# Local attention and group whitening on one core: the last sub-image taken by channel half

## The chip, the core and the metric

The kernel runs on one core of a Trainium2 chip. The core has a matrix engine (TensorE, PE in the profile, with its weight loads as PEld), three engines for elementwise work (VectorE or DVE, ScalarE or ACT, GpSimd or POOL), SyncE (SP), which here only issues transfers, and 16 DMA engines. Matrix products land in PSUM[...]; only VectorE and ScalarE bring them from there to SBUF. The metric is the time of the program on the device, in microseconds, as the median of several runs; the profile is of one execution.

## The reference

The input x has 4 images of 256 channels, 64 x 64 pixels. Two layers follow one another.

```python
k = conv7x7_dilated2(x, w1) + b1          # 256 -> 128 channels
k = conv1x1(k, w2) + b2                   # 128 -> 49
attn = softmax(k, axis=1)                 # 49 weights for each pixel
y = einsum('bkchw,bkhw->bchw', shifts(x), attn)   # weighted sum of 49 shifted pixels

x = y as (g=4 groups, 64 channels, all pixels of all images)
xc = x - mean
Sigma = EPS * I + xc xc^T / m             # one 64 x 64 matrix for each group
rTr = 1 / trace(Sigma);  S = Sigma * rTr;  P = I
for _ in range(5): P = 1.5 * P - 0.5 * (P P P) S
out = (P * sqrt(rTr)) xc * weight + bias
```

The whitening needs the moments of all pixels of all four images before the first result can be written. The four groups are independent of each other.

## The kernel before

The dilated convolution works on row and column parities, with a transform that saves products; it fills most of the 686 us and isn't touched. Softmax gives the 49 weights of each pixel; they are written to memory and read back as banded matrices (`band`, and `bandz` for the edge between the two row halves), so that the weighted sum of a sub-image is a product of a block of transposed pixels with a band.

There are 16 sub-images (n = 0 to 15, four for each image, by row and column parity). A sub-image is worked on in `first_half` and `second_half`, its two row halves (the argument `half`). `make_blocks` (L1243) transposes pixels on TensorE (L1250) and copies them out as xb (L1281) and as edge blocks xbz (L1272). `weighted_sum` (L1296) adds one of five pieces of a row half into the PSUM tile y (L1313): four block pieces and an edge piece, each for the 128 channels `cc` = 0 and for `cc` = 1. These are the channel halves, two groups each. `store_y` (L1323) adds a pivot and puts y in its slot: ScalarE for channel half 0 (L1334), VectorE for half 1 (L1332) in the last three sub-images. `turn_y` (L1340) transposes the stored y again (L1346) and copies it to a buffer yt (L1356); `moments` (L1361) multiplies it with itself (L1371) and sums everything into the PSUM tile `sig`, which holds both channel halves side by side. A sub-image's second row half is turned, and its moments taken, within the next one's first row half; for the last, `finish` (L1402) does it.

After that `whiten(cc)` (L1629) is a generator, cut into steps by `yield`. From `sig` it forms the mean, the trace and S, then runs four rounds of two products with an eviction each (L1634 and L1685 are the copy and the update that ends a round), and at the end the scale and the offset (`sc`, `beta`). For channel half 0, `run_on` (L1622) puts products of the unit matrix into a PSUM tile `still` between the steps. The first step of half 1 comes after half 0's first round; its others are taken one by one in the output loop by `others`.

The output loop goes through the channel halves and images. It makes 32 tiles of 128 channels x 16 rows: products of the whitening matrix with the slots (L1615), for the two row parities; one is evicted by ScalarE (L1757), one by VectorE (L1761), into a ring of six SBUF tiles (tag `out`), and SP stores the tile (L1764). The PSUM pairs rotate over `apply` (both banks of one tile), `cv` and `tp` (two tiles each).

The order of TensorE's work is the order of the program (`pe` keeps it). A planner orders the work of the other engines by its estimates and by data; `high_priority` brings an instruction forward, and `issue_after` puts it behind another one. Each engine works off its own queue in order. The PSUM pool of y has one buffer, that of tp three.

## Time and profile before

| what | value |
|---|---|
| median of three runs | 688.17 us (687.89 to 688.29) |
| the profiled execution | 688.48 us, span 686.5 us |
| TensorE busy | 652.2 us (95% of the span) |
| VectorE / ScalarE busy | 567.1 us / 329.4 us |
| transfers of the result, L1764 | 32 of 512 KB, 5.7 us each from issue to landing |
| granted TensorE clock | 0.995 |

How to read it: times in the trace are microseconds from the start of the span. A row of the timeline has start, duration, engine, line, operation, result <- operands, shapes, count, and in brackets the idle time before it and what ended it. A row that gathers several instructions lasts from the first one's start to the last one's end. A float32 product is two instructions in the rows. A row of the chain has start, share of the chain in microseconds, engine, what and line; "issue" is time in which the engine waited for nothing that the profile shows. A busy TensorE isn't a TensorE doing needed work.

### The profile page before, as it was taken

To read this page: it belongs to the slowest core of one execution; us is meant where nothing else is said; L and a number is where in the kernel's file an instruction comes from. 1 tells how busy PE (TensorE), PEld (TensorE's weight loads), DVE (VectorE), ACT (ScalarE), POOL (GpSimd) and SP (SyncE) were. 2 spreads that over 40 slices of the span, in tenths; PEclk is the share of its full clock that TensorE was granted. 3 is DMA by queue.
4 is the path that set the end of the run, shared out by engine and by line. 5 is a ranking of instruction groups with operands and counts; after the bars stand their busy time and mean duration, and the time that the engine had idled before them with its cause. 6 is when DMAs were issued, how large, how long until landed. Compare 5 with 4: busy or idle time off the path is not lost.

```text
span 686.5 us, 19090 instructions
## 1 busy us (share of the span) xinstructions
PE 652.2 (95%) x7820; PEld 530.6 (77%) x7820; DVE 567.1 (83%) x1245; ACT 329.4 (48%) x849; POOL 117.4 (17%) x177
## 2 busy tenths in 40 slices
PE   6999999999999999999899999999999999999983
PEld 1439572367899998899899998999899998997320
DVE  2799999999489889999999499989998987433663
ACT  1424240023565564566754454464754656543463
POOL 0000551652222020002121200010220212400000
PEclk9999999999999999999999999999999999999997
DMA  8951999992699989222588493036462426646598
GB/s 318 246 155 66 143 265 354 219 182 38 151 192 220 209 194 365 86 90 74 151 267 275 108 325 116 6 94 169 137 177 73 98 48 155 166 147 284 223 405 353
DMA packets 110463, 126.09 MB, mean 184 GB/s; under 512 B 69239, under 2 KB 91880, under 8 KB 109224
## 3 DMA queue, kind: packets, MB, share of 16 engines
q1 hardware_dynamic: 93384, 69.03, 34.7%
q0 software_dynamic: 10944, 37.57, 21.7%
q10 hardware_dynamic: 6048, 18.27, 8.7%
q8 instruction: 61, 1.00, 0.6%
q14 instruction: 26, 0.21, 0.1%
HBM read 78.78 MB, written 52.36 MB: 191 GB/s over the span
## 4 chain that ended last, share of the span: by engine, by line
PE 68%; DVE 20%; ACT 6%; DMA 3%; issue 2%; DVEq 0%; ACTq 0%; POOL 0%; SPq 0%; POOLq 0%
PE cv L603 24%; PE y L1313 11%; PE cv L770 8%; PE acc L770 8%; PE tp L1346 3%; PE sig L1371 3%; PE tp L1250 3%; DVE pv L352 2%; DVE zz L352 2%; PE cv L251 2%; DVE xh L352 2%; DMA out_dram<-out 2%; DVE ct L352 2%; DVE zz L348 1%; DVE zz L345 1%
## 5 line engine op out<-in xcount | busy, mean ns | idle before, releaser
L603 PE MATMUL cv<-xh,wr 128*49 128x128 f32 x4160 | 232.5, 273 | 0.3 <-ACT pv L614 0.2
L603 PEld LDWEIGHTS cv<-xh,wr 128*49 128x49 f32 x4160 | 226.1, 124 | 3.4 <-issue 1.0
L1145 POOL DMA_DIRECT2D sd<-zt x124 | 65.4, 534 | 333.6 <-ACT zt L1126 268.5
L1313 PE MATMUL y<-band,xb 128*128 128x209 f32 x480 | 100.7, 342 | 5.3 <-ACT xb L1281 2.7
L1313 PEld LDWEIGHTS y<-band,xb 128*128 128x128 f32 x480 | 81.2, 191 | 6.6 <-ACT xb L1281 3.3
L614 ACT COPY pv<-cv 113x486 f32<-113x486 f32 (+2 forms) x60 | 25.9, 432 | 86.1 <-PE cv L603 85.8
L352 DVE SCALAR_TENSOR_TENSOR pv<-pv 113x162 f32<-113x162 f32 x176 | 52.8, 321 | 2.1 <-ACT pv L614 1.4
L1356 ACT COPY yt<-tp 128x512 f32<-128x512 f32 x64 | 37.2, 593 | 25.1 <-PE tp L1346 24.7
L1346 PE MATMUL tp<-ident,slot 128*128 128x128 f32 x256 | 45.5, 298 | 1.6 <-ACT slot L1334 1.2
L1126 ACT COPY zt<-d 32x112 f32<-32x112 f32 (+2 forms) x132 | 38.5, 291 | 15.5 <-DVE d L996 9.9
L1346 PEld LDWEIGHTS tp<-ident,slot 128*128 128x128 f32 x256 | 37.6, 206 | 7.8 <-issue 3.7
L1048 ACT ACTIVATE d<-tp,mx 128x49 f32<-128x49 f32 x96 | 27.5, 323 | 28.3 <-DVE mx L1045 28.3
L1250 PE MATMUL tp<-ident,slot 128*128 128x128 f32 x256 | 40.6, 282 | 0.0
L1371 PE MATMUL sig<-yt 128*64 128x65 f32 x1024 | 37.4, 225 | 1.8 <-ACT yt L1356 1.8
L1250 PEld LDWEIGHTS tp<-ident,slot 128*128 128x128 f32 x256 | 38.3, 206 | 0.2 <-issue 0.2
L1371 PEld LDWEIGHTS sig<-yt 128*64 128x64 f32 x1024 | 32.7, 137 | 6.3 <-ACT yt L1356 2.8
L352 DVE SCALAR_TENSOR_TENSOR xh<-ct 128x512 f32<-128x512 f32 x40 | 26.6, 693 | 10.3 <-PE cv L603 10.2
L1281 ACT COPY xb<-tp 128x512 f32<-128x512 f32 x52 | 30.6, 588 | 8.8 <-PE tp L1250 5.7
L770 PE MATMUL acc<-slot,tap 128*49 128x256 f32 (+7 forms) x224 | 34.7, 468 | 0.0
L770 PEld LDWEIGHTS acc<-slot,tap 128*49 128x49 f32 x224 | 16.1, 123 | 17.9 <-issue 15.5
L147 POOL DMA_DIRECT2D slot<-in_x_dram x12 | 20.4, 1701 | 54.1 <-DVE xh L352 38.6
L348 DVE TENSOR_TENSOR pv<-pv 113x162 f32<-113x162 f32 (+1 forms) x77 | 27.5, 365 | 0.3
(255 smaller groups left out, 1127.2 us busy)
## 6 DMA issues: line engine op xcount, KB each, us to landing
out_dram<-out SPq DMA_DIRECT2D x32, 512.0 KB, 5.7
band<-sd SPq DMA_DIRECT2D x64, 242.0 KB, 3.7
sd<-zt POOLq DMA_DIRECT2D x124, 77.0 KB, 3.2
wr<-gd ACTq DMA_DIRECT2D x14, 588.0 KB, 4.9
wr<-gd ACTq DMA_DIRECT2D x14, 490.0 KB, 5.3
slot<-in_x_dram POOLq DMA_DIRECT2D x12, 512.0 KB, 10.3
ahead<-in_x_dram POOLq DMA_DIRECT2D x12, 512.0 KB, 7.6
spill<-slot POOLq DMA_DIRECT2D x3, 2048.0 KB, 11.2
```

Of the source, the lines that this page charges most:

```text
L348: return in_turn(TT(o, a, b, ALU.subtract))
L352: return in_turn(STT(o, a, f, b, ALU.mult, ALU.add))
L603: nc.tensor.matmul(o, wv[:, sc, sr, cc], xv[bc][:, h * NCC + cc], start=(j == 0), stop=(j == len(terms) - 1), skip_group_check=True,)
L770: nc.tensor.matmul(ps[h * HB : h * HB + KT, :, o0:o1], w[v][:, cc], rhs, start=(j == 0 and k == 0), stop=(j == len(order) - 1), skip_group ...
L1126: ins = nc.scalar.copy(o, i)
L1145: dma = queue.dma_start(bass.AP(tensor=D.tensor, offset=D.offset + h * HS + g * RS, ap=[[LS, TC], [CR * RS, NCH], [1, KS * WS]],), zt[p0 : ...
L1250: nc.tensor.transpose(t[:, h * C + cc * P : h * C + (cc + 1) * P], tile_of(xt, cc, t8, h, pc), turned_by(n),)
L1281: (nc.vector.tensor_copy if n > 4 * B - 3 else nc.scalar.copy)(xb.rearrange("p a c -> p (a c)"), t[:, : 2 * C])
L1313: nc.tensor.matmul(ps[:, cc, q0 : q0 + nq, c0:c1], xb[:, cc * P : (cc + 1) * P], rhs, start=(k == 0), stop=(k == len(PIECES[half]) - 1), s ...
L1346: nc.tensor.transpose(t[:, h * C + cc * P : h * C + (cc + 1) * P], tile_of(yt, cc, t8, h, pc), turned_by(n),)
L1356: return nc.scalar.copy(yb.rearrange("p h a g c -> p (h a g) c")[:, :, :GW], t[:, : 2 * C].rearrange("p (e c) -> p e c", c=GW),)
L1371: nc.tensor.matmul(sig[g * GW : (g + 1) * GW, cc], yb[:, cc, g, :GW], yb[:, cc, g], start=(count[0] == 0), stop=(count[0] >= NCC * 4 * B * ...
```

## The change

The last sub-image (n = 15) gets an order of its own, by channel half. All weighted sums, turns and moments of channel half 0 come first, with two of the ten sums of half 1 behind the last turn. The rest of half 1 is cut into eleven units, which `whiten(0)` takes at the places where `run_on` stood; `run_on` and `still` go. Its y tile now holds the two row halves of one channel half, its block copies lie in tiles of the output ring so that they last, and stores and turned copies are split between ScalarE and VectorE (some units use one engine alone). Sub-images 13 to 15 order the copy of some blocks behind VectorE's store of y. In the whitening's start, two steps go to ScalarE and the sign of the mean moves; a square root is taken early, on a value that isn't used. The offset is made before the output loop. The first output tile is cut in two of 8 rows each, VectorE's first evictions are kept in order, and the second whitening starts behind output tile 4 and goes on by one step with each tile from number 6.

```diff
...
-    def make_blocks(n, t8):
+    LAST = 4 * B - 1
+    def make_blocks(n, t8, after=None):
...
                 )
-        if n == 4 * (B - 1):
+        if n in (4 * (B - 1), LAST):
             if t8 % 2 == 0:
                 ahead_xb.append(
-                    rpool.tile([P, 4, C], F32, tag="out", name=f"xbs_{t8}", bufs=6)
+                    rpool.tile([P, 4, C], F32, tag="out", name=f"xbs_{n}_{t8}", bufs=6)
                 )
...
             edges()
-        with tc.high_priority():
+        with tc.high_priority(), tc.issue_after(after.ins) if after else nullcontext():
             (nc.vector.tensor_copy if n > 4 * B - 3 else nc.scalar.copy)(
...
-    def weighted_sum(n, half, k):
+    def weighted_sum(n, half, k, ccs=range(NCC)):
         m = PIECES[half][k]
-        if k == 0:
-            y_ps[n, half] = ps_y.tile([P, NCC, HALF, SW], F32, tag="y", name=f"y_{n}_{half}")
-        ps = y_ps[n, half]
+        if n < LAST:
+            if k == 0:
+                y = ps_y.tile([P, NCC, HALF, SW], F32, tag="y", name=f"y_{n}_{half}")
+                for cc in ccs:
+                    y_ps[n, half, cc] = y[:, cc]
+        elif (half, k) == (0, 0):
+            y = ps_y.tile([P, 2, HALF, SW], F32, tag="y", name=f"y_{n}_{ccs[0]}")
+            for o in range(2):
+                y_ps[n, o, ccs[0]] = y[:, o]
         xb = blocks[n, m]
...
         yt, pc = where(n)
-        ps = y_ps.pop((n, half))
         shift = pivots[place(n)[1]]
...
             o = halves(yt)[:, cc, :, half * HALF : (half + 1) * HALF, bass.ds(pc, TC, 2)]
-            i = ps[:, cc].rearrange("p r (h c) -> p h r c", h=2)
+            i = y_ps.pop((n, half, cc)).rearrange("p r (h c) -> p h r c", h=2)
             with tc.high_priority():
                 if n > 4 * (B - 1) and cc:
-                    nc.vector.tensor_scalar(o, i, shift[:, cc : cc + 1], None, ALU.add)
+                    y_dve[n, half] = nc.vector.tensor_scalar(
+                        o, i, shift[:, cc : cc + 1], None, ALU.add
+                    )
                 else:
...
+    y_dve, y_act = {}, {}
+    def store_part(half, cc, both=True):
+        yt, pc = where(LAST)
+        shift = pivots[place(LAST)[1]][:, cc : cc + 1]
+        ps = y_ps.pop((LAST, half, cc)).rearrange("p r (h c) -> p h r c", h=2)
+        for h in range(2):
+            o = halves(yt)[:, cc, h, half * HALF : (half + 1) * HALF, bass.ds(pc, TC, 2)]
+            with tc.high_priority():
+                if h and both:
+                    y_dve[LAST, half] = nc.vector.tensor_scalar(
+                        o, ps[:, h], shift, None, ALU.add
+                    )
+                else:
+                    y_act[0] = nc.scalar.activation(o, ps[:, h], AF.Identity, bias=shift)
+    def turn_part(half, cc, to=None, on=(nc.scalar.copy, nc.vector.tensor_copy)):
+        yt, pc = where(LAST)
+        t = tp()
+        for k in range(4):
+            pe(
+                nc.tensor.transpose(
+                    t[:, k * P : (k + 1) * P],
+                    tile_of(yt, cc, 2 * half + k // 2, k % 2, pc),
+                    turned_by(LAST),
+                )
+            )
+        to = cc if to is None else to
+        for k in range(2):
+            with tc.high_priority():
+                on[k](
+                    yt_buf[k][:, :, to, :, :GW],
+                    t[:, k * C : (k + 1) * C].rearrange("p (h g c) -> p h g c", h=2, c=GW),
+                )
+        turned_part[half, cc] = [yt_buf[k][:, h, to] for k in range(2) for h in range(2)]
+    turned_part = {}
+    def moments_part(half, cc, pieces=range(4), end=False):
+        for k in pieces:
+            moment(turned_part[half, cc][k], cc, end and k == 3)
...
+    def moment(yb, cc, end=False):
+        for g in range(P // GW):
+            pe(
+                nc.tensor.matmul(
+                    sig[g * GW : (g + 1) * GW, cc],
+                    yb[:, g, :GW],
+                    yb[:, g],
+                    start=(count[0] == 0),
+                    stop=end,
+                    skip_group_check=True,
+                )
+            )
+        count[0] += 1
...
-        pieces = [(i, cc) for i in range(4 * half, 4 * half + 4) for cc in range(NCC)]
-        if (n, half) == (4 * B - 1, 1):
-            pieces.sort(key=lambda p: p[1])
...
+        for i in range(4 * half, 4 * half + 4):
+            for cc in range(NCC):
+                moment(ybs[n, i][:, cc], cc)
...
         load_band(n + 1, 0)
-        block(3)
+        make_blocks(n, 3, y_dve.get((n, 0))) if (n, (3, 0)) not in blocks else None
         if last is not None:
...
         if n + 1 < 4 * B:
-            make_blocks(n + 1, 0)
+            make_blocks(n + 1, 0, y_dve.get((n, 1)))
         moments(n, 0)
...
     soft_rows(1, 1)
-    for f in rest[5:]:
+    for f in rest[5:-2]:
         f()
-    finish()
+    def sums(half, cc, *ks):
+        for k in ks:
+            weighted_sum(LAST, half, k, (cc,))
+    prev = open_n.pop()
+    turn_y(prev, 2)
+    sums(0, 0, 0)
+    make_blocks(LAST, 1)
+    sums(0, 0, 1)
+    make_blocks(LAST, 2)
+    sums(0, 0, 2)
+    turn_y(prev, 3)
+    sums(0, 0, 3, 4)
+    store_part(0, 0)
+    make_blocks(LAST, 3, y_dve[LAST, 0])
+    moments(prev, 1)
+    root = work.tile([P, 1], F32, tag="root", name="root")
+    with tc.issue_after(y_act[0].ins):
+        nc.scalar.activation(root, cmask[:, :1], AF.Sqrt)
+    turn_part(0, 0)
+    sums(1, 0, 0, 1, 2, 3, 4)
+    store_part(1, 0)
+    moments_part(0, 0)
+    turn_part(1, 0)
+    sums(0, 1, 0, 1)
+    moments_part(1, 0, end=True)
+    units = [
+        lambda: sums(0, 1, 2, 3),
+        lambda: (sums(0, 1, 4), store_part(0, 1, False)),
+        lambda: sums(1, 1, 0, 1, 2),
+        lambda: sums(1, 1, 3),
+        lambda: (sums(1, 1, 4), store_part(1, 1)),
+        lambda: turn_part(0, 1),
+        lambda: turn_part(1, 1, 0, [nc.vector.tensor_copy] * 2),
+        lambda: moments_part(0, 1, (0, 1)),
+        lambda: moments_part(0, 1, (2, 3)),
+        lambda: moments_part(1, 1, (0, 1)),
+        lambda: moments_part(1, 1, (2, 3), True),
+    ]
...
-    still = ps_y.tile([P, 2, 512], F32, tag="y", name="still")
-    def run_on(k):
-        for _ in range(k):
-            pe(nc.tensor.matmul(still[:, 0, :P], ident, ident, start=True, stop=True))
-    latest = []
...
-        fill = run_on if cc == 0 else (lambda k: None)
+        def fill():
+            if cc == 0:
+                units.pop(0)()
...
         G = sig[:, cc]
-        mu = work.tile([P, 1], F32, tag="mu", name=f"mu{cc}")
-        nc.vector.tensor_scalar(mu, G[:, GW : GW + 1], 1.0 / NPIX, None, ALU.mult)
+        nmu = work.tile([P, 1], F32, tag="nmu", name=f"nmu{cc}")
+        nc.scalar.mul(nmu, G[:, GW : GW + 1], -1.0 / NPIX)
         D = small(f"D{cc}")
-        nc.vector.tensor_scalar(D, own, mu, None, ALU.mult)
-        if cc == 0:
-            t = tp()
-            fill(1)
-            pe(nc.tensor.matmul(t[:, :GW], blk, D, start=True, stop=True))
-        nmu = work.tile([P, 1], F32, tag="nmu", name=f"nmu{cc}")
-        nc.vector.tensor_scalar(nmu, mu, -1.0, None, ALU.mult)
+        nc.scalar.activation(D, own, AF.Copy, scale=nmu)
         dt_ = small(f"dt{cc}")
...
         nc.vector.tensor_reduce(dg, dt_, AX.X, ALU.add)
+        mu = work.tile([P, 1], F32, tag="mu", name=f"mu{cc}")
+        nc.vector.tensor_scalar(mu, G[:, GW : GW + 1], 1.0 / NPIX, None, ALU.mult)
         nc.vector.tensor_scalar(dg, dg, 1.0 / NPIX, EPS, ALU.mult, ALU.add)
         nc.vector.scalar_tensor_tensor(dg, mu, nmu, dg, ALU.mult, ALU.add)
+        fill()
         if cc:
             yield
-            t = tp()
-            pe(nc.tensor.matmul(t[:, :GW], blk, D, start=True, stop=True))
-        fill(2)
+        t = tp()
+        pe(nc.tensor.matmul(t[:, :GW], blk, D, start=True, stop=True))
+        fill()
         pe(nc.tensor.matmul(t[:, GW : GW + 1], blk, dg, start=True, stop=True))
...
         nc.vector.scalar_tensor_tensor(S, G[:, :GW], 1.0 / NPIX, eps, ALU.mult, ALU.add)
-        nc.vector.scalar_tensor_tensor(S, t[:, :GW], nmu, S, ALU.mult, ALU.add)
+        nc.vector.scalar_tensor_tensor(S, t[:, :GW], mu, S, ALU.mult, ALU.add)
         rtr = work.tile([P, 1], F32, tag="rtr", name=f"rtr{cc}")
...
     chains = [whiten(cc) for cc in range(NCC)]
-    for _ in range(3):
-        next(chains[0])
-    with tc.issue_after(latest[0].ins):
-        next(chains[1])
-    while 0 not in wm:
+    while 0 not in beta:
         next(chains[0])
...
-    def others():
-        for chain in chains:
-            if next(chain, "done") != "done":
-                break
+    LEAD = 4
+    evicted = {}
...
     pair = bank_pairs()
+    idx = -1
     for cc in range(NCC):
         for b in (3, 2, 1, 0):
-            for q in range(SH // TR):
-                st = rpool.tile([P, TR, 2, W], F32, tag="out", name=f"out_{b}_{cc}_{q}", bufs=6)
+            rows = [(q, TR) for q in range(0, SH, TR)]
+            if (cc, b) == (0, B - 1):
+                rows[:1] = [(0, TR // 2), (TR // 2, TR // 2)]
+            for k, (r0, nr) in enumerate(rows):
+                idx += 1
+                st = rpool.tile([P, TR, 2, W], F32, tag="out", name=f"out_{b}_{cc}_{r0}", bufs=6)
+                st = st[:, :nr]
                 ts = next(pair)
                 for pr in range(2):
-                    y = halves(slots[2 * b + pr])[:, cc, :, q * TR : (q + 1) * TR, :]
+                    y = halves(slots[2 * b + pr])[:, cc, :, r0 : r0 + nr, :]
                     parts_mm(
-                        ts[pr],
+                        ts[pr][:, : nr * W],
                         (wmx if pr else wm)[cc],
...
                     )
-                others()
+                if idx > LEAD + 1:
+                    next(chains[1], None)
                 for pr in range(2):
                     o = st[:, :, pr, :].rearrange("p r (h w) -> p h r w", h=2)
-                    i = ts[pr].rearrange("p (h r w) -> p h r w", h=2, w=SW)
-                    if pr == q % 2:
-                        nc.scalar.activation(
+                    i = ts[pr][:, : nr * W].rearrange("p (h r w) -> p h r w", h=2, w=SW)
+                    if pr == k % 2:
+                        on_act = nc.scalar.activation(
                             o, i, AF.Identity, bias=beta[cc], scale=sc[cc]
...
                     else:
-                        nc.vector.tensor_scalar(
-                            o, i, sc[cc], beta[cc], ALU.mult, ALU.add
-                        )
+                        behind = evicted.get(idx - 1) if idx <= LEAD else None
+                        with tc.issue_after(behind.ins) if behind else nullcontext():
+                            evicted[idx] = nc.vector.tensor_scalar(
+                                o, i, sc[cc], beta[cc], ALU.mult, ALU.add
+                            )
+                if idx == LEAD:
+                    with tc.issue_after(evicted[idx].ins), tc.issue_after(on_act.ins):
+                        next(chains[1])
                 nc.sync.dma_start(
-                    out[b, cc * P : (cc + 1) * P, 2 * q * TR : 2 * (q + 1) * TR, :],
+                    out[b, cc * P : (cc + 1) * P, 2 * r0 : 2 * (r0 + nr), :],
                     st.rearrange("p r two w -> p (r two) w"),
...
```

## The prediction

> **What bounds the kernel now.** I read the page first (TensorE busy 95% of the span, DMA 3% of the chain), then busy time by stretch over the last 86 us, the chain in order of time, and the timeline where the chain changes engine. Columns of the stretches: length, busy of PE, PEld, DVE, ACT, POOL, then clock, DMA share, GB/s.
>
> ```profile
> 625.00:630.00 5.00, 4.27 (x76) 3.45 (x70) 1.52 (x8) 2.94 (x4) 0.00 (x0) 1.00 0.85 364
> 630.00:635.00 5.00, 4.68 (x40) 3.54 (x41) 3.26 (x22) 0.73 (x3) 0.00 (x0) 1.00 0.04 16
> 635.00:640.00 5.00, 4.94 (x44) 2.58 (x44) 1.41 (x7) 0.87 (x4) 0.00 (x0) 1.00 0.00 0
> 642.00:644.00 2.00, 1.40 (x19) 0.58 (x22) 1.80 (x8) 0.61 (x2) 0.00 (x0) 1.00 0.89 363
> 646.00:648.00 2.00, 2.00 (x26) 0.72 (x24) 1.33 (x5) 1.58 (x3) 0.00 (x0) 1.00 0.81 315
> 656.00:676.00 20.00, 15.28 (x136) 4.92 (x136) 13.17 (x18) 11.45 (x17) 0.00 (x0) 1.00 1.02 406
> ```
>
> From about 642.2 to 684.3 us the transfers of the result (32 x 512 KB, 16.8 MB) run at about 405 GB/s; 16.8 MB at that rate is 41.4 us, so little is lost there. Nothing behind the first result byte can be shortened much; the end moves with the time of that byte. Ten microseconds before it the transfer engines are idle and TensorE is "busy". With what, the chain says:
>
> ```profile
> 628.27 0.94 PE sig L1371 x24
> ...
> 629.24 0.16 DVE mu L1638
> ...
> 632.39 0.42 PE still L1625 x2
> 632.81 0.27 PE tp L1615 x4
> 633.07 0.42 PE still L1625 x2
> ...
> 640.20 1.53 DVE out L1761 x2
> ```
>
> The last moment is in at 629.21; the whitening chain runs to the last update of its matrix (629.24 to 637.90, 8.7 us), with products of the unit matrix (`still`, L1625) filling TensorE; from 637.90 to the first byte (642.2) it is 4.3 us more. Two details of the timeline matter below.
>
> ```profile
> 605.47 0.69 DVE L1281 COPY xb<-tp 128x512 f32<-128x512 f32 x1 [1.03 <-PE tp L1250]
> 606.08 0.74 DVE L1332 TENSOR_SCALAR slot<-y,pivot 128x512 f32<-128x512 f32 x1
> 606.45 1.06 PE L1346 MATMUL tp<-ident,slot 128*128 128x128 f32 x4
> ...
> 624.85 0.74 ACT L1334 ACTIVATE slot<-y,pivot_x 128x512 f32<-128x512 f32 x1 [1.49 <-PE y L1313]
> 625.62 0.75 DVE L1332 TENSOR_SCALAR slot<-y,pivot_x 128x512 f32<-128x512 f32 x1 [5.25 <-ACT slot L1334]
> ...
> 628.24 1.28 ACT L1696 ACT_TABLE_LOAD   x1
> ```
>
> First: VectorE does the block copy before the store of y, and the transposes of y (1.06 us instead of 0.63) wait. Second: the two stores of y are strictly one after the other, though they read two banks of the tile y.
>
> **The change, part by part.** Half means channel half (0 or 1) here, as in the change's words.
>
> *Order of copy and store.* The block copy now follows VectorE's store of y. In the three places of sub-images 13 to 15 where both are on VectorE (598, 605.5, 611.8) the store starts at ScalarE's end instead of 0.35 to 0.75 later. At 606 the transposes then don't stall: 1.06 - 0.63, but only 0.33 after the overlap with the moments. At the other two the next sum waits for the later copy instead, so about 0.12 and 0.11 remain. What is queued behind the store is this copy; its readers are the next sums, and that is the loss just counted. For sub-image 13 the copy is on ScalarE and is read some 3 us later: nothing. Gain **0.55 us** (0 to 0.8).
>
> *Last sub-image by halves, before the whitening.* Pitches on TensorE: a block piece for both halves 0.71 (chain, 4 instructions), so 0.357 for one; an edge piece 0.42, so 0.21; four transposes 0.47; 32 moment instructions 1.1. Half 1's ten pieces are 8 x 0.357 + 2 x 0.21 = 3.28; two of them (0.71) stay ahead of the whitening, so 2.57 leave; with 8 transposes (0.94) and half of the moments (1.1) it is 4.6 us. The stalls change as well. Before, 619.99 to 629.21 holds 9.22 us for 7.4 us of work (16 transposes 1.9, sums 3.3, moments 2.2): 1.85 us of stalls. After, I lay it out: sums of half 0 end about 620.3 (on the old clock, without the gain above); store 0.51 on ScalarE (0.736 less 256 elements at the 0.83 ns that the rows of 512 and 256 elements, 587 and 367 ns, give) and then 0.48 on VectorE; 16 moments (0.55) cover part, so the transposes wait 0.5; their eviction (0.37 then 0.42, the 256-element rows of both engines) lies beside the two sums of half 1, with 0.2 left over. Stalls 0.7, 1.15 less. Up to the end of half 0's moments: **-5.75 us**, with the order -6.3.
>
> The copies of all four blocks now stay in two tiles of the output ring (six buffers, two were used before for sub-image 12): the ring is empty then, no wait.
>
> *The square root's table, placed early.* It is 1.28 us on ScalarE behind the store at about 617.5, before the eviction of the first half's transposes, ready 618.7: 0.3 late, with the sums (1.65 us) as cover, so nothing. The Trainium skill (ScalarE: Activation LUTs, What ACT_TABLE_LOAD costs) speaks against that: it puts a drain of about 1.38 us beside the load, 2.66 in all. ScalarE would then come free near 620.4, the eviction and the next store would shift, and the second transposes start 0.4 later. The trace shows only the 1.28 row, with ScalarE idle behind it until 631.29, so it can't exclude the drain; I take nothing and keep 0.4 for the range.
>
> *First whitening with real work as its filler.* 14 unit products (28 instructions, 0.42 us each product) go; 11 units come. Front: the first unit is 0.71; `D` now comes from ScalarE (two small ones, 0.2 and 0.24 by the rows of q and wmx) inside it; VectorE's sums on the diagonal wait for ScalarE's first reading of the same tile, then take about 0.9, ending near 1.15; unit two (0.21) ends there too. Before, the second product came 1.55 after the last moment; now 1.2. That gains 0.35.
> Unit two also issues two stores of half 1 on ScalarE, 1.0 us, from the lower bank of y, and unit three (0.92 us of sums) writes the upper bank of the same tile. The skill (PSUM — Partial Sum Buffer, PSUM bank collisions raise a hardware error) forbids two engines only the same bank in the same quadrant: by it unit three starts at once and the front keeps its 0.35. The trace shows more: at 624.85 and 625.62 two readers of *different* banks of one tile follow each other, and so do all pairs on the tile `apply`, never those on cv and tp, which are tiles of their own:
>
> ```profile
> 655.57 0.81 DVE L1761 TENSOR_SCALAR out<-apply,ab 128x512 f32<-128x512 f32 x1 [1.07 <-ACT out L1757]
> ...
> 663.32 0.78 ACT L1757 ACTIVATE out<-cv,ab 128x512 f32<-128x512 f32 x1 [0.45 <-DMA out_dram<-out]
> 663.63 0.80 DVE L1761 TENSOR_SCALAR out<-cv,ab 128x512 f32<-128x512 f32 x1
> ```
>
> If a matmul is held the same way (no row shows it), unit three starts 1.05 after unit two and the front *loses* 0.5. I take the loss, as the nearest row is that one; ends +0.35 and -0.5.
> Iterations: a step is now bound by the round trip (0.35 us from matmul end to the next matmul), not by 0.42 of filler; units of 0.36 and 0.28 fit, the two transpose units (0.47) don't (0.1 each), and the third iteration's bank of the ring of three waits for an eviction, 0.2. Against 5.95 before I take 6.15 (5.6 to 8.2, see the rivals). Whitening in all: **+0.7 us**.
>
> *First tile in two, offsets first.* After the last update: the offset's matmuls 0.3; half a tile of matmuls about 0.6 (half of 638.10 to 639.24); ScalarE 0.57, VectorE 0.54, one after the other as the tile is `apply`; with gaps 2.05; then 0.5 to the first byte as before (641.73 to 642.22). 2.55 against 4.3: **-1.75 us**. The offset is ready (0.8) before the matmuls are, so it is hidden. The second half follows 0.55 later, within the 0.65 that 256 KB take at 405 GB/s. SP issues one transfer more, 33 (0.7 us each), beside the stream.
>
> *Second whitening from tile 4 on.* Before it stole from VectorE while the stream was young (315 GB/s at 646); in all 0.7 us was lost. Now five tiles go first: by 0.8 us of eviction per tile against 1.29 of transfer the stream gains a lead of some two tiles before the first step. Gain **0.3** (-0.7 to +0.6).
>
> Sum: -6.3 + 0.7 - 1.75 - 0.3 = -7.65 us on the profiled execution (span 686.5, 688.48 with what lies around it). The median of the runs is 688.17, 0.3 below; I carry the difference over: **680.5 us**, span near 678.9.
>
> **Rivals.** (1) *Everything hides:* no hold on unit three, iterations at 5.6: 0.85 + 0.55 better, 679.1. For: the round trip 0.35; against: the serial readers. (2) *The evictions in the units become the chain:* the four units with stores or transposes put a 0.5 us item ahead of the chain's own copy or update in ScalarE's or VectorE's queue, each in its turn: +2.0, 682.5. For: both queues are in order and the stores come in the same microsecond as the copies; against: the chain's items are emitted first in most steps. (3) *Slower:* the second whitening starves the stream. Its eleven steps are tied to tiles 6 to 16, one each; a tile that takes over 1.29 us delays the last byte once the lead is used. To eat 7.65 us each of eleven must take 1.29 + 0.7 = 1.99 us; at 2.2 it is 11 x 0.91 = 10 us, 690.5. Against: with the steps in it before, 642 to 650 went at 366 GB/s, 1.43 us a tile. (4) *The change doesn't do what it says:* the readings of half 0's moments wait for half 1's as well, since both lie in one tile (`sig`); before, `mu` of half 0 started at 629.24 only after the last moment of half 1, at 629.21. Then only the first tile's 1.75 and the order's 0.55 are left, 685.9. Against: in the new program half 1's matmuls come behind those readings. The reloading of the slots isn't in the way: it ends near 629.5, five microseconds before the first byte.
>
> **How the numbers follow.** The case summed 0.55 (own range 679.6 to 681.5), (1) 0.18, (2) 0.22, (3) 0.03, (4) 0.02, half of which lies within 0.2%. The range goes from the low side of (1) to beyond (2), with the drain added: 678.8 to 683.3. A difference below 0.2% (1.4 us) can't be told from none here. Faster 0.96, same 0.01, slower 0.03.
>
> **What would show it.** Half 0's last moment near 622.9; the last update 9.4 later, at 632.3; first byte near 634.8; the stream then at 405 GB/s without a hole. The hold shows as TensorE idle 0.8 us ahead of unit three, released by ScalarE. No `still` rows. Wrong if the last update comes after 634 (case 2), or stretches under 370 GB/s lie between tiles 6 and 16 (case 3).

## The result and the profile after

The changed kernel takes **683.23 us** (five runs, 682.56 to 685.45) against 688.29 us (five runs, 687.89 to 690.32) for the kernel before, run beside it: a ratio of 0.9928, 95% interval 0.9904 to 0.9953. In a later group of runs on another chip it was 0.9945 (0.9921 to 0.9969). It is faster, by about 5 us instead of the 7.65 us that were forecast, and the time lies outside the range of the likeliest case and almost at the top of the wide one.

The profiled executions have spans of 686.5 and 681.3 us. To compare stretches I count from a marker that the change doesn't touch: the start of a block of 32 moment instructions of an earlier sub-image, near 569 us. It starts 0.42 us sooner in the profile after (569.02 against 569.44), which isn't the change's doing. All that follows is in distances from there. The first three stretches repeat to 0.05 us between executions of programs that are alike up to there; the last two are read from windows of a quarter of a microsecond, to about 0.1 us.

| stretch, us | before | after | change | forecast |
|---|---|---|---|---|
| marker to `dt`, an early reading of half 0's moments ("first reading" below) | 59.87 | 54.77 | -5.10 | -6.3 |
| front, to the first round's product | 2.64 | 3.22 | +0.58 | +0.5 |
| rounds, to the last update | 5.95 | 6.69 | +0.74 | +0.2 |
| last update to first byte | 4.28 | 3.07 | -1.21 | -1.75 |
| stream: first byte to the end of the full rate | 41.99 | 42.37 | +0.38 | -0.3 |
| sum | 114.73 | 110.12 | -4.61 | -7.65 |

Every row but the front has a share in the 3.0 us that are missing: 1.2, 0.5, 0.5 and 0.7. Three remarks on the rows:

- The very first reading (`mu` before, `nmu` after) lies 0.07 us ahead of `dt` before and 0.20 after. Counted from the end of the last moment, as the prediction counts, the first row is -5.2 and the front +0.7.
- The first packet of the result starts at 642.22 and 636.71, 4.32 and 3.02 us behind the last update: -1.30 by that count.
- The stream ends here where its full rate ends. Behind it comes a tail of 0.9 to 1.4 us, not the same in every execution, in which the DMA engines run empty (after: busy 47% in 679.00 to 679.25, 17% in the next quarter, then 6%). To the end of the last packet the change brings 4.76 us (115.79 to 111.03).

The chain of work that ended last, after, in the last sub-image and the whitening (start, share of the chain, engine, what, line):

```profile
613.75 0.70 DVE xbs L1282
...
614.48 0.37 ACT xbz L1273
...
620.42 0.50 ACT slot L1360
...
620.95 0.49 DVE slot L1356
...
622.82 0.72 PE sig L1418 x16
...
624.98 0.86 ACT slot L1360 x2
...
625.88 1.20 PE y L1320 x6
627.08 0.37 PE tp L1708 x4
627.45 0.55 PE y L1320 x2
...
629.18 0.67 PE tp L1368 x4
...
631.16 0.38 PE sig L1418 x8
...
633.80 0.22 PE tp L1708 x4
```

There is no `still` any more: its place is taken by sums (y, 0.55), transposes (tp L1368, 0.67) and moments (sig, 0.38). At 624.98 ScalarE's two stores are on the chain; that is the hold, TensorE's wait ahead of unit three. The timeline of the same execution shows the copies of blocks, the table load, the first reading, the hold and the first tile:

```profile
614.48 1.50 ACT L1273 COPY xbz<-tp 64x256 f32<-64x256 f32 x4 [1.15 <-DVE xbs L1282]
...
616.03 0.30 PEld L1320 LDWEIGHTS y<-bandz,xbz 128*128 128x128 f32 x2 [0.41 <-ACT xbz L1273]
...
617.04 1.28 ACT L1666 ACT_TABLE_LOAD   x1
618.33 0.20 ACT L1666 ACTIVATE root<-cmask 128x1 f32<-128x1 f32 x1
...
623.59 0.17 ACT L1724 ACTIVATE nmu<-sig 128x1 f32<-128x1 f32 x1 [1.01 <-PE sig L1418]
...
624.98 0.85 ACT L1360 ACTIVATE slot<-y,pivot_x 128x256 f32<-128x256 f32 x2 [0.84 <-PE y L1320]
...
625.88 0.46 PE L1320 MATMUL y<-bandz,xbz 128*128 128x96 f32 x2 [0.67 <-ACT slot L1360]
...
634.70 0.56 ACT L1837 ACTIVATE out<-apply,ab 128x256 f32<-128x256 f32 x1 [0.73 <-PE apply L1708]
...
635.30 0.54 DVE L1843 TENSOR_SCALAR out<-apply,ab 128x256 f32<-128x256 f32 x1 [0.81 <-ACT out L1837]
...
635.87 0.83 SPq L1849 DMA_DIRECT2D out_dram<-out  x2
```

Busy time by stretch (the columns are those of the prediction: length, PE, PEld, DVE, ACT, POOL, clock, DMA share, GB/s) shows two holes in the stream, at its start and at 646, and TensorE little busy at 642:

```profile
632.00:634.00 2.00, 1.96 (x39) 1.42 (x39) 0.79 (x4) 0.51 (x2) 0.00 (x0) 1.00 0.00 0
636.00:638.00 2.00, 2.00 (x20) 0.72 (x24) 1.83 (x3) 0.72 (x2) 0.00 (x0) 1.00 0.66 247
642.00:644.00 2.00, 1.16 (x17) 0.64 (x19) 1.64 (x7) 1.45 (x3) 0.00 (x0) 1.00 0.98 385
646.00:648.00 2.00, 1.77 (x21) 0.40 (x13) 2.00 (x6) 0.91 (x2) 0.00 (x0) 1.00 0.78 307
660.00:670.00 10.00, 8.09 (x76) 2.54 (x70) 7.01 (x9) 6.21 (x9) 0.00 (x0) 1.00 1.02 406
```

### The profile page after: what moved, and what is told of

It is laid out like the page before. It is cut to its first block, busy times and chain, and to the rows that moved or that the text cites. A ratio compares the mean times of both kernels' runs of the same rounds, so it can differ in the third digit from the quotient of the medians.

```text
span 681.3 us, 19062 instructions
## 1 busy us (share of the span) xinstructions
PE 648.7 (95%) x7800; PEld 527.3 (77%) x7800; DVE 568.4 (83%) x1248; ACT 330.4 (48%) x857; POOL 117.2 (17%) x177
## 4 chain that ended last, share of the span: by engine, by line
PE 66%; DVE 20%; ACT 6%; DMA 4%; issue 2%; POOL 0%; ACTq 0%; SPq 0%; DVEq 0%; POOLq 0%
PE cv L603 22%; PE y L1320 11%; PE cv L770 8%; PE acc L770 8%; PE sig L1418 4%; PE tp L1399 3%; PE tp L1251 3%; DVE pv L352 2%; DVE zz L352 2%; PE cv L251 2%; DVE xh L352 2%; DMA out_dram<-out 2%; DVE ct L352 2%; DVE zz L348 1%; ACT d L1048 1%
## 5 line engine op out<-in xcount | busy, mean ns | idle before, releaser
L1320 PE MATMUL y<-band,xb 128*128 128x209 f32 x448 | 94.0, 342 | 5.0 <-ACT xb L1282 2.7
L1320 PEld LDWEIGHTS y<-band,xb 128*128 128x128 f32 x448 | 75.7, 190 | 6.5 <-ACT xb L1282 3.3
L1409 ACT COPY yt<-tp 128x512 f32<-128x512 f32 x60 | 35.0, 593 | 19.4 <-PE tp L1399 19.0
L1399 PE MATMUL tp<-ident,slot 128*128 128x128 f32 x240 | 41.5, 296 | 1.2 <-ACT slot L1342 1.2
L1251 PE MATMUL tp<-ident,slot 128*128 128x128 f32 x256 | 40.5, 282 | 0.0
L1399 PEld LDWEIGHTS tp<-ident,slot 128*128 128x128 f32 x240 | 34.9, 205 | 6.3 <-issue 3.7
L1251 PEld LDWEIGHTS tp<-ident,slot 128*128 128x128 f32 x256 | 38.2, 204 | 0.2 <-issue 0.2
```

The costliest lines, as they stand in the source:

```text
L1251: nc.tensor.transpose(t[:, h * C + cc * P : h * C + (cc + 1) * P], tile_of(xt, cc, t8, h, pc), turned_by(n),)
L1320: nc.tensor.matmul(y_ps[n, half, cc][:, q0 : q0 + nq, c0:c1], xb[:, cc * P : (cc + 1) * P], rhs, start=(k == 0), stop=(k == len(PIECES[hal ...
L1399: nc.tensor.transpose(t[:, h * C + cc * P : h * C + (cc + 1) * P], tile_of(yt, cc, t8, h, pc), turned_by(n),)
L1409: return nc.scalar.copy(yb.rearrange("p h a g c -> p (h a g) c")[:, :, :GW], t[:, : 2 * C].rearrange("p (e c) -> p e c", c=GW),)
```

## The experiments

My theory after the result: the mechanisms are those of the prediction, and four of its terms have the wrong size. The rivals: the evictions in the units hold the rounds (case 2 of the prediction), and the stream is starved by the second whitening (case 3). The stretches of all runs, in us, counted as above; "full rate" is the distance from the marker to the end of the full rate, "last packet" that to the end of the last packet; the ratio is that to the kernel before in the same group of runs:

| run | first reading | front | rounds | first byte | stream | full rate | last packet | median, ratio |
|---|---|---|---|---|---|---|---|---|
| before | 59.87 | 2.64 | 5.95 | 4.28 | 41.99 | 114.73 | 115.79 | |
| after | 54.77 | 3.22 | 6.69 | 3.07 | 42.37 | 110.12 | 111.03 | 683.23, 0.9928 |
| e1_upper_in_cv | 54.75 | 2.50 | 6.68 | 3.06 | 42.36 | 109.35 | 110.31 | 682.81, 0.9912 |
| e2_units_first | 61.74 | 2.52 | 7.03 | 3.56 | 43.83 | 118.68 | 119.97 | 693.48, 1.0055 |
| e3_first_tile_whole | 54.76 | 3.22 | 6.69 | 3.88 | 42.71 | 111.26 | 112.53 | 683.51, 0.9912 |
| e4_order_alone | 59.11 | 2.64 | 5.95 | 4.30 | 41.93 | 113.93 | 115.04 | 687.29, 0.9986 |
| e5_units_first_filled | 61.75 | 2.61 | 5.94 | 3.03 | 42.39 | 115.72 | 116.85 | 688.97, 1.0018 |
| e6_no_second_whitening | 54.76 | 3.23 | 6.67 | 3.07 | 41.68 | 109.41 | 110.81 | 683.84, 0.9934 |
| e7_two_tiles_first | 54.79 | 2.49 | 6.69 | 2.51 | 42.56 | 109.04 | 110.25 | 682.54, 0.9913 |
| e8_small_units | 54.78 | 2.50 | 6.33 | 2.46 | 43.11 | 109.18 | 110.50 | 681.65, 0.9905 |
| e9_best | 54.67 | 2.50 | 6.33 | 2.47 | 43.92 | 109.89 | 111.17 | 686.17, 0.9951 |
| e10_second_from_tile_0 | 54.77 | 3.22 | 6.68 | 3.19 | 43.09 | 110.95 | 112.10 | 686.67, 0.9955 |
| e11_edges_ordered | 54.67 | 3.22 | 6.69 | 3.02 | 42.36 | 109.96 | 111.10 | 685.25, 0.9937 |
| a0_after (changed kernel again) | 54.78 | 3.22 | 6.68 | 3.08 | 43.76 | 111.52 | 112.46 | 685.24, 0.9945 |

Half widths of the ratios' intervals are 0.0010 to 0.0028, so most variants of the changed kernel can't be told apart by their times; the stretches can. In the last group the changed kernel's median is 2 us higher, which goes with TensorE's clock (last section): its executions with a mean granted clock of 0.995 or more took 683.5 and 684.0 us, those below 684.7 to 687.9.

**The hold.** The upper half of half 1's sums goes to a bank of the tile `cv`, which is a tile of its own, and no longer to the other bank of the tile y.

```diff
...
+            if ccs[0]:
+                y_ps[n, 1, 1] = cv_buf[0].rearrange("p (r c) -> p r c", c=SW)
```

> The sums of the upper row half of channel half 1 go to a PSUM tile of their own (the first cv tile) instead of the second bank of y. Theory (hold): a matmul is kept off a tile while another engine reads any bank of it; then the 0.67 us in which TensorE waited for ScalarE ahead of unit three is gone, the first round starts 0.85 us sooner after the last moment of half 0 (2.7 instead of 3.54 us), and the time is about 0.8 us below the changed kernel. Rival (the wait is for something else, the buffers of the transposes or ScalarE's queue): the wait stays, and the time is that of the changed kernel.

The front falls from 3.22 to 2.50, the time from the marker to the last packet by 0.72. The timeline of e1: the matmuls start 0.10 us after the stores instead of 0.90.

```profile
625.23 0.86 ACT L1362 ACTIVATE slot<-y,pivot_x 128x256 f32<-128x256 f32 x2 [0.84 <-PE y L1322]
...
625.33 0.44 PE L1322 MATMUL cv<-bandz,xbz 128*128 128x96 f32 x2
```

So a matmul waits for readers of another bank of the same tile (y is one tile of two banks, `cv` are two tiles of one bank each), and with that wait gone the front is 0.14 better than before, where the prediction had 0.35. The bank read and the bank written are different ones in both kernels, and what differs is the tile; that speaks for the framework's tracking of tiles as the cause, but these runs don't show it.

**Units ahead of the whitening, then with the old filler.** Both take the eleven units in one go before the whitening starts. The first leaves its rounds bare, the second fills them with products of the unit matrix as the kernel before did.

```diff
...
         def fill():
-            if cc == 0:
-                units.pop(0)()
+            pass
...
+    for f in units:
+        f()
     chains = [whiten(cc) for cc in range(NCC)]
```

> All eleven units stand ahead of the first whitening, which then runs with nothing between its steps. Theory (each filler costs its first weight load, 0.1 to 0.2 us, besides its matmuls): the four rounds take 5.5 to 5.7 us instead of 6.62, the front about 2.3 instead of 3.54, so the whitening is 2.2 us shorter; but the 5 us of matmuls and some 1 us of stalls come before it: first result byte about 3.5 to 4 us later than in the changed kernel, time near 687. Rival (the fillers are free and the rounds are bound by VectorE and ScalarE): the rounds stay above 6.4 us and the time is near 689.

```diff
...
+        counts = [1, 2, 3] + [1] * 8
+
         def fill():
             if cc == 0:
-                units.pop(0)()
+                for _ in range(counts.pop(0)):
+                    pe(nc.tensor.matmul(still[:, 0, :P], ident, ident, start=True, stop=True))
...
+    for f in units:
+        f()
+    still = ps_y.tile([P, 2, 512], F32, tag="y", name="still")
```

> As the kernel with the units ahead of the whitening, but with the old products of the unit matrix (14 of them, in the old places) between its steps, so that TensorE's clock has no cause to fall. Theory (the gain is the units' work under the whitening, and a filler costs its first weight load besides its matmuls): the clock stays at 1.00, the front takes 2.6 to 2.8 us and the four rounds 5.9 to 6.0, against 3.54 and 6.62 in the changed kernel; the units in a row cost 7.0 us, so the first byte comes 5.5 us later, time 688.5. Rival (what made the other kernel slow was not the clock but the units' stores in a row): the rounds stay above 6.6 us with the clock at 1.00.

The first missed its expectation by 6 us. Busy time by stretch of e2 says why: TensorE was at work 40% of 632 to 636 us, and then its clock was halved for ten microseconds (0.50 to 0.52 in all windows from 636 to 646).

```profile
632.00:634.00 2.00, 0.79 (x4) 0.59 (x4) 1.42 (x9) 0.49 (x2) 0.00 (x0) 1.00 0.00 0
634.00:636.00 2.00, 0.80 (x10) 0.45 (x10) 1.09 (x7) 0.32 (x2) 0.00 (x0) 1.00 0.04 8
636.00:638.00 2.00, 1.31 (x10) 0.73 (x12) 0.42 (x2) 0.27 (x1) 0.00 (x0) 0.52 0.00 0
```

The Trainium skill (TensorE: Matmul & The Clock Gate, What's actually happening) says that the clock is halved after an idle window of about 3.4 us; the 4 us here agree in length, though TensorE was partly at work in them. So a filler is needed, and e2 says nothing on the evictions. e5 does: clock 1.00, rounds 5.94, 688.97 us against 688.5 expected. The units cost the rounds 0.75 us (6.69 - 5.94). Comparing e5 with e4, the order by halves *costs* 2.64 us (61.75 against 59.11) as long as half 1's work stays ahead of the whitening, with the waits between its units in that sum; taking that work into the whitening brings 6.98.

**First tile whole.**

```diff
...
-            if (cc, b) == (0, B - 1):
-                rows[:1] = [(0, TR // 2), (TR // 2, TR // 2)]
```

> The first result tile is not cut in two. By the prediction's working half a tile saves 0.3 us of matmuls, 0.21 and 0.27 of evictions: the first byte comes 0.8 us later than in the changed kernel and the end with it, about 0.8 us more. Rival: the stream's first microseconds have slack in both kernels (holes of about 1 us lie between tiles 4 and 12), so that the later first byte is won back and the time is the same within 0.3 us.

The first byte comes 0.81 us later, and the stream is 0.34 longer; in that execution the clock fell at 643.0, with TensorE idle for 40% of 640 to 642 (busy time by stretch of e3):

```profile
640.00:642.00 2.00, 1.20 (x8) 0.80 (x12) 1.49 (x7) 1.29 (x2) 0.00 (x0) 1.00 1.01 399
...
644.00:646.00 2.00, 2.00 (x16) 0.76 (x13) 1.04 (x6) 0.26 (x1) 0.00 (x0) 0.50 1.03 397
```

In the medians the 0.8 us can't be seen (683.51 in its group).

**The order of copy and store alone**, in the kernel before:

```diff
...
-        block(3)
+        make_blocks(n, 3, y_dve.get((n, 0))) if (n, (3, 0)) not in blocks else None
...
-            make_blocks(n + 1, 0)
+            make_blocks(n + 1, 0, y_dve.get((n, 1)))
```

> The kernel before with only the block copies of sub-images 13 to 15 ordered behind VectorE's store of y. Prediction's step: 0.55 us faster than before, with the transposes at 599, 606 and 613 no longer waiting; it can hardly be told from none by the clock, but by the trace: first sum of sub-image 15 about 0.55 us earlier, counted from the last moments of sub-image 11. In sub-image 15's own second half nothing stands in VectorE's way. Rival: the later block copy delays the next sums by the same amount: 0.

0.9986 (0.9976 to 0.9996), and 0.76 us in the trace. Of these 0.32 are at a fourth place, within the last sub-image: four transposes at 619.99 took 0.90 from start to start in the kernel before and take 0.58 here. At the three places of the prediction it is 0.44.

**No second whitening.** Both channel halves use half 0's matrix, scale and offset: the whitening of half 1 is left out.

```diff
...
+    for table in (wm, wmx, sc, beta):
+        table[1] = table[0]
...
-                if idx > LEAD + 1:
-                    next(chains[1], None)
...
-                if idx == LEAD:
-                    with tc.issue_after(evicted[idx].ins), tc.issue_after(on_act.ins):
-                        next(chains[1])
```

> Leaves out the whitening of channel half 1: its tiles are made with half 0's matrix, scale and offset. Theory (the second whitening's steps hold TensorE and VectorE up in tiles 6 to 16, and the stream, whose lead is under two tiles, runs dry): the stretch of 307 GB/s goes, the stream takes 41.5 us from first to last byte instead of 42.4, time 682.4. Rival (the holes come from the transfers themselves, or from the serial evictions on the tile apply): the holes stay and the time is that of the changed kernel, 683.2.

The stream takes 41.68 instead of 42.37 us; the tail gives part of that back, and to the last packet it is 0.22 us. The median, 683.84, doesn't show the 0.7; in the profiled execution the clock fell at 334 us, ahead of the marker. All that the second whitening takes from the stream is thus 0.7 us or less. The stretch of 307 GB/s at 646, the sign that the prediction named for case 3, is there after the change and gone here (380 to 414 in all windows from 640 to 658), so case 3 is real in kind; in size, 7.65 us, it is refuted.

**The second whitening without a lead:** first step behind tile 0 instead of 4.

```diff
-    LEAD = 4
+    LEAD = 0
```

> The changed kernel with the second whitening's steps behind tiles 0 to 12 instead of 4 on. Theory that the lead of four tiles matters: the early steps take VectorE and TensorE from a young stream, which becomes longer, 42.6 to 43.2 us against 42.37, and the time 0.3 to 0.8 longer, 683.5 to 684.0. Rival, the steps cost the stream the same wherever they stand: 42.37 and 683.2.

The stream becomes 43.09, as the theory had it; the hole is at 642 (e10, busy time by stretch):

```profile
642.00:644.00 2.00, 1.96 (x27) 0.60 (x24) 1.68 (x6) 1.73 (x3) 0.00 (x0) 1.00 0.35 135
```

The lead is worth 0.72 us in this kernel (1.07 to the last packet). The medians (686.67 against 685.24 for the changed kernel in the same group) point the same way, but their intervals overlap.

**First tiles on separate PSUM tiles.** e1's edit, and the PSUM pairs come in the order cv, tp, apply.

```diff
...
         while True:
-            t = ps_y.tile([P, 2, NT], F32, tag="y", name="apply")
-            yield [t[:, k] for k in range(2)]
             yield cv_buf
             yield [tp(), tp()]
+            t = ps_y.tile([P, 2, NT], F32, tag="y", name="apply")
+            yield [t[:, k] for k in range(2)]
```

> The changed kernel with the upper row half of channel half 1 in the first cv tile, and the first two half tiles of the result on the pairs cv and tp, whose two banks are tiles of their own, instead of apply and cv. Theory (two readers of one PSUM tile are kept apart): ScalarE and VectorE evict the first half tile at once, the first byte comes 0.5 us sooner after the last update (2.5 us instead of 3.0), on top of the 0.72 of the separate tile: 1.2 us below the changed kernel's first byte, time 682.0. Rival (the later tiles then run dry, since the whole third tile now waits for the serial pair): the gain is lost in a hole behind the second half tile, time 682.7.

The two evictions of the first half tile now run side by side (timeline of e7; after, the same pair stood at 634.70 and 635.30), and the first byte comes 0.56 us sooner after the last update than in the changed kernel:

```profile
633.90 0.56 ACT L1839 ACTIVATE out<-cv,ab 128x256 f32<-128x256 f32 x1 [0.62 <-PE cv L1710]
634.02 0.54 DVE L1845 TENSOR_SCALAR out<-cv,ab 128x256 f32<-128x256 f32 x1 [0.21 <-PE cv L1710]
```

But the stream is 0.20 longer than e1's (42.56), with 206 GB/s from 636 to 638, and to the last packet only 0.06 of e1's time is gained: the rival of this run, a hole behind the second half tile, is in part right.

**Small units.** On top of e7: the two units of four transposes become four of two, and half 1's last moments go from the rounds to the place ahead of tile 3.

```diff
...
-        lambda: turn_part(0, 1),
-        lambda: turn_part(1, 1, 0, [nc.vector.tensor_copy] * 2),
+        lambda: turn_pair(0, 1, 0, 1),
+        lambda: turn_pair(0, 1, 1, 1),
+        lambda: turn_pair(1, 1, 0, 0),
+        lambda: turn_pair(1, 1, 1, 0),
...
-        lambda: moments_part(1, 1, (0, 1)),
-        lambda: moments_part(1, 1, (2, 3), True),
...
+                if idx == 2:
+                    moments_part(1, 1, range(4), True)
```

> As the one with two tiles first, and the units cut by what a step leaves free: transposes by twos (0.19 + 0.24 us) in four steps, evicted by ScalarE, moments of half 1's lower rows in two, and those of its upper rows behind the third tile's matmuls. Theory (a filler costs 0.19 us for its first weights besides its matmuls, and what exceeds the round trip lengthens the round): the second and third round take 1.5 us each instead of 2.0 and 1.45, all four 6.2 instead of 6.62, first byte another 0.4 sooner, time 681.6. Rival (rounds are bound elsewhere): 6.6 us, no change.

Rounds 6.33, and 681.65 us, the shortest median of all, though not apart from e7's. The chain of e8 shows a unit of two transposes and a unit of eight moments:

```profile
628.52 0.44 PE tp L1682 x2
...
631.67 0.38 PE sig L1420 x8
```

Two transposes cost 0.44, four 0.67. Four without interruption are 0.47, so there is a fixed price of 0.20 us, whatever the number of transposes; eight moments pay 0.10 (0.38 against 0.28). But the stream is now 43.11: from 636 to 638 us it moved 210 GB/s, and from 644 to 648 it moved 320 and 346. In the profile e8 ends 0.25 us later than e7; that execution was the slowest of its four.

**Everything together.** On top of e8: two tiles in halves instead of one, half 1's last moments behind tile 4, one more tile of lead, and e11's order of the edges.

```diff
...
-    LEAD = 4
+    LEAD = 5
...
-                rows[:1] = [(0, TR // 2), (TR // 2, TR // 2)]
+                rows[:2] = [(r, TR // 2) for r in range(0, 2 * TR, TR // 2)]
...
-                if idx == 2:
+                if idx == 4:
                     moments_part(1, 1, range(4), True)
```

> The small units and the first two tiles in four halves on cv, tp, apply; half 1's last moments behind the fifth tile instead of ahead of the fourth; the second whitening one tile later; the halves' edge pieces in the order of their use. Theory that the hole of 1 to 2 us just behind the first byte comes from the moments ahead of tile 3 and from the serial tile apply: stream 42.4 or less (43.11 in the run with small units before this one), first reading 54.5 (54.78), rounds 6.33, first byte 2.5 behind the last update: about 681.0 us, 2.2 below the changed kernel. Rival, the transfers themselves start slowly: the stream stays at 43.1 and the time at 681.5.

Both expectations missed: the early hole is gone, and two later ones took its place, so that the stream is longer still, 43.92 (busy time by stretch of e9):

```profile
636.00:638.00 2.00, 2.00 (x32) 1.06 (x32) 1.37 (x4) 0.78 (x2) 0.00 (x0) 1.00 0.99 365
...
640.00:642.00 2.00, 0.55 (x3) 0.42 (x4) 1.83 (x6) 1.18 (x3) 0.00 (x0) 1.00 0.81 326
...
644.00:646.00 2.00, 1.75 (x24) 0.57 (x20) 2.00 (x6) 1.24 (x3) 0.00 (x0) 1.00 0.29 104
```

The first byte is 65.97 us behind the marker, against 67.75 in the changed kernel, but the end of the full rate only 0.23 sooner, and the last packet 0.14 later. From e7 over e8 to e9 the first byte comes 0.4 and 0.1 us sooner and the end of the full rate 0.1 and 0.7 *later*: with fewer tiles ahead, it seems, the evictions around the second whitening's first step can't keep up with the transfers. The median is 686.17 beside 685.24 of the changed kernel in the same group: nothing gained. No version here has a shorter median than e8 and e7, and these two are not told apart from e1 by time or by last packet (110.25 to 110.50).

**The edges' order.** ScalarE copies the edge that half 0's sums need first ahead of the other one.

```diff
...
+                late = edge_of.get(2) if n == LAST and t8 == 1 else None
-                with tc.high_priority():
+                with tc.high_priority(), tc.issue_after(late.ins) if late else nullcontext():
```

> The changed kernel with one order more: ScalarE copies the edge that half 0's sums need before the one that half 1's need. Theory that the halves' order uncovered this copy: the edge piece no longer waits, and the first reading of half 0's moments comes 54.5 us behind the moments of sub-image 11 (54.77 in the changed kernel); 682.9 us. Rival, the wait only moves to the next eviction: 54.75 and 683.2.

In between: 0.10 us of the hoped-for 0.27. The sum's edge piece comes straight behind the sum now, and part of the wait goes to the next transposes (timeline of e11):

```profile
616.04 0.35 PE L1321 MATMUL y<-bandz,xbz 128*128 128x96 f32 x2
...
616.41 0.74 PE L1251 MATMUL tp<-ident,slot 128*128 128x128 f32 x4
```

**The changed kernel again**, without an edit, beside e9 to e11:

> The changed kernel once more, beside the others of this group. Both theories: about 683.2 us, ratio 0.9928; the stretches as in its first profile: moments of sub-image 11 to the first reading of half 0's moments 54.8 us, front of the whitening 3.22, rounds 6.69, last update to first byte 3.07, stream 42.4.

All stretches up to the first byte repeat to 0.01 us. The stream doesn't, 43.76 against 42.37, and the marker comes 2.98 us later. Together these are the 4.4 us between the two spans (685.7 and 681.3), and both go with falls of the clock, as the last section shows.

## Why the prediction was partly wrong

**Last sub-image by halves: the term "stalls 0.7, 1.15 less" failed.** The work that leaves was right: from start to start of the rows, the sums' stretch shrinks by 3.18 us from e4 to the changed kernel where whole pieces and transposes make 3.75, and the rest by 1.24 where they make 0.84. The 0.7 us of stalls that I laid out behind the sums measured 0.87. What I left out lies *ahead of* them: between 612.62 and 616.91 the sums now lose 0.66 us in waits of 0.1 to 0.24, and in e4 0.11. With both halves a piece lasts 0.71 us and covers a copy of a block (0.69 on VectorE), and the chain of e4 stays on TensorE from 610.9 to 623.6; with one half it lasts 0.36, and the chain after goes through VectorE's copy at 613.75 and the four edge copies on ScalarE (1.50 us at 614.48), for whose end the edge piece waits at 616.03. That these copies are behind all of the 0.66 is argued: e11 moved one of them and won 0.10. So the stalls from e4 on are 0.55 more and 0.40 less, not 0.83 less. (0.32 of the 1.15 is the order's fourth place, e4.) This is the largest miss, 1.2 us in the table's first row with 0.1 of the order and 0.1 for `dt`, which stands later behind the last moment. (Two slips in the working: the rows named for 0.83 ns an element give 0.86, and 9.22 less 7.4 is 1.82. The first store measured 0.49 against 0.51; neither matters.)

**Order of copy and store.** 0.55 forecast, 0.44 at the places named: right. It brought 0.32 more at a place that the prediction didn't see (e4).

**The front.** The hold was foreseen rightly, from the nearest row, but the sum fits better than its parts: 0.85 was taken for the hold, and e1 takes 0.72 away; the 0.35 to be gained ahead of it came out as 0.14, and as 0.03 when counted from the last moment. +0.5 forecast and +0.58 measured agree in part by luck. The rule of the Trainium skill weighed there (PSUM — Partial Sum Buffer, PSUM bank collisions raise a hardware error) would have let unit three start at once, since it writes another bank; the row at 625.88 and e1 decide for the wait.

**Rounds: "units of 0.36 and 0.28 fit" failed.** They don't: their pitch isn't their price. The chain through the rounds lies on TensorE alone, but for 0.04 us twice, so it is not the evictions either (case 2). The last update came at 633.70, 1.4 after the forecast and just ahead of the 634 that was to show case 2; that the time came out 0.7 from case 2's 682.5 is chance. A sum unit takes 0.55 instead of 0.36, four transposes 0.67 instead of 0.47, eight moments 0.38 instead of 0.28. Against eight times 0.42 of `still` that is 2 x 0.55 + 2 x 0.67 + 4 x 0.38 = 3.96, or +0.6 of the measured 0.74; the third bank's wait of 0.2 didn't show. e8 shows the price of transposes to be fixed for each unit. What it is stays open. The matrix chain uses 64 x 64 quarters of the array and the units more of it, and the Trainium skill (TensorEngine Tiling (Array Packing), Key Properties) says that a change of tiling mode drains TensorE, without a figure. The expectations of e2, e5 and e8 name a rival, the first weight load of a unit, and it fits the sizes as well: the loads of sums, transposes and moments last 0.19, 0.21 and 0.14 us on the page of the kernel before. No run here parts the two. The old filler paid it too: it took 0.42 for two instructions of 128 columns, and four such instructions take 0.47 in the transposes. So I had the price in front of me and read it as the filler's own length.

**First byte: the step "then 0.5 to the first byte as before" failed.** I measured from the eviction that ended at 641.73, that of `apply`. SP's queue sent the tile from `cv` first: its evictions ended at 641.35, the issue is at 641.38, ahead of the end of `apply`'s, and the first packet started at 642.22, 0.87 us behind the eviction (timeline of before):

```profile
640.58 0.77 ACT L1757 ACTIVATE out<-cv,ab 128x512 f32<-128x512 f32 x1
...
640.93 0.80 DVE L1761 TENSOR_SCALAR out<-apply,ab 128x512 f32<-128x512 f32 x1
...
641.38 0.81 SPq L1764 DMA_DIRECT2D out_dram<-out  x2
```

After, it is 635.84 to 636.71, 0.87 again. The evictions themselves ended 2.14 after the last update, forecast 2.05. The two together, 0.46, are the whole miss when the first packet is counted (3.02 against 2.55).

**Second whitening from tile 4: "gain 0.3" failed.** The stream lost 0.38. The lead does help (e10: 0.72), but the whitening's first steps used to run within the first whitening and around the first byte and now stand in the stream, 2.5 to 6 us behind it: TensorE is busy 1.16 of 2 us at 642. I counted the steps by tile and not what was moved. Without the whitening the stream would take 41.68 (e6), so the most to gain was 0.3 against before, all of which the forecast claimed. That the place of the first steps makes the 0.38 is argued from these rows; no run has the changed kernel with the steps where they were before.

**The table load.** 1.28 us, and ScalarE's next instruction starts 0.01 us after it (617.04 and 618.33). The drain of 1.38 us that the Trainium skill (ScalarE: Activation LUTs, What ACT_TABLE_LOAD costs) puts beside it doesn't show here; taking nothing was right.

**Cases 1 and 4.** The hold and the rounds exclude the first. The fourth is excluded too: `nmu` reads half 0's moments at 623.59, ten microseconds before half 1's last ones.

## What to carry to other kernels

A stretch that is halved also halves what it covers: list the copies that ran beneath it before subtracting its work. A filler's price is its distance in the chain, from start to start, not its own matmuls; here each unit of sums or transposes had a fixed part of 0.2 us, of moments 0.1. Bringing the first byte forward doesn't pay by itself: from e7 to e9 it came 0.5 us sooner and the end later. The last byte, not the first, is to be watched.

## What the hardware showed unexpectedly

Most of the scatter between executions goes with the clock, and one place is far from the change. At 328 to 334 us TensorE waits for a band's transfer: 2.3 us in the first profile after, 2.6 in that of before, 2.6 in a0, 3.1 in e6. In the last two the clock then fell to half, for 6.8 and 3.4 us, in the first two it didn't. In all traces such a fall ahead of TensorE's last work lasts 3.41 us or two or three times that. Busy time by stretch of a0, where the last two lines are the stream:

```profile
330.00:332.00 2.00, 1.36 (x8) 1.17 (x8) 2.00 (x8) 1.98 (x6) 0.00 (x0) 0.99 0.97 362
332.00:334.00 2.00, 1.16 (x3) 1.14 (x4) 2.00 (x7) 0.74 (x2) 0.00 (x0) 0.50 1.05 307
334.00:336.00 2.00, 2.00 (x9) 1.84 (x9) 2.00 (x6) 0.50 (x2) 0.00 (x0) 0.50 0.77 217
...
644.00:646.00 2.00, 1.06 (x14) 0.21 (x10) 1.93 (x7) 1.10 (x2) 0.00 (x0) 1.00 1.01 406
646.00:648.00 2.00, 2.00 (x17) 0.87 (x16) 0.79 (x3) 0.44 (x2) 0.00 (x0) 0.50 0.96 373
```

In the executions with the fall (a0, e2, e6, e10) the marker stands at 570.3 to 572.0 us, in all others at 568.2 to 569.6: 1 to 3 us in a place where the kernels are alike. It is enough to hide any edit worth less, and it is why the stretches decide here and not the medians.

The second fall, at 646, is closer to the change: the same program at clock 0.50 and 0.65 needs 43.76 us for the stream instead of 42.37. TensorE had been busy for 1.06 of the 2 us before, in the second whitening's first step. The busy share of two microseconds doesn't decide it alone: it was 0.55 of 2 us at 640 in e9 and 0.18 at 650 in e6, and no fall followed. The two profiles without the moved step, before and e4, have no such fall in the stream; of those with it a0 and e3 have one. So the moved step seems to carry a risk, 1.4 us in a0, that neither the sum nor the rivals had.
